# Running 20 of 23 expert tiles always, and the last three inside one branch

## The chip, the core and the metric

The kernel runs on one core of a Trainium2 chip. The metric is the device time of one execution in microseconds; the median of several runs is compared. The engines are called PE (matrix multiplication, with its weight loads shown as PEld), DVE (vector), ACT (scalar and activation), POOL (general purpose, here also the issuer of indirect transfers) and SP (the issuer of nearly all other transfers).

## What is computed

The reference is a two-layer decoder over x of shape (4, 256, 256), so 1024 rows of 256. Layer 0 is a windowed attention, a cross attention on 1601 context rows, and a ternary feed-forward block. Layer 1 is a latent attention, a linear cross attention and a mixture of experts. Each of the six blocks ends with a residual sum and a normalisation of each row. Only the last block matters here:

```
logits  = 30 * tanh((x @ w_gate) / 30)         # (1024, 8)
probs   = softmax(logits)
weights = probs, kept for the two largest of each row, 0 elsewhere
for e in range(8):
    h   = silu(x @ w1[e]) * (x @ w3[e])        # (1024, 512)
    out = out + (h @ w2[e]) * weights[:, e]    # (1024, 256)
x = layernorm(x + out)
```

Each row needs only two of the eight experts, so there are 2048 pairs of a row and an expert.

## The kernel before, in words

The kernel doesn't issue instructions as it is written. It records operations in a `Loom`, each with its engine, an estimated time, the buffers that it reads and writes and a priority. At the end `weave` puts them into one order by a small planner: of all operations that could go next, it takes the one that can start earliest, by the estimates, and on a tie the one of higher priority. That order is the order on each engine's queue. `hold_order(False)` lets the framework place the instructions that follow by its own rule until `hold_order(True)`. A buffer of a pool has a tag, and `room` and `take` hand out its places. Because all operations go through helpers, the profile shows most of them with the helper's line: L261 for matmuls, L268 for transposes, L275 for transfers issued by SP, L398 for DVE, ACT and POOL operations.

The mixture of experts is done by sorting rows into lists. After the cross attention of a batch, `route` finds each row's two experts, counts the rows of each expert in the running count `nxt`, and scatters the row (256 values, its gate and its slot) into the expert's list in DRAM (`lists`). A tile is 128 rows of one list. Since eight lists may each end with a partly filled tile, up to `TILES = 2 * T // P + NE - 1` = 23 tiles may be needed; how many really are depends on the routing. The kernel before always runs 23.

`tile_table` makes a table with one entry for each tile: an expert's number and the first row in its list. It is called three times. The first call, when three of the four batches have been routed, covers 5 tiles; the second, after seven eighths of the rows, 2 more; these two take only tiles that are already full. The last call covers the remaining `LATE` = 16. In it `nt` is the number of tiles that each expert still needs and `upto` its running sum over the experts; entries past the last needed tile point to rows that hold nothing.

`expert_tile` does one tile. Its steps are:

- on SP, a register load of the list's row from the table, and the fetch of the rows (`xg`, L1407 to L1409); a register load of the expert's number and two transfers with w1 and w3 of that expert (`wt`, 4 buffers, L1416 to L1421);
- on PE, a register load of the expert's number, two transposes of `xg` into a bank, copied to `xgT`; then matmuls of `xgT` with `wt` into two banks;
- tanh on ACT and two products on DVE, which give `eh`;
- on PE, matmuls of `eh` with `w2e`, which holds w2 of all experts, addressed with the expert's register;
- on DVE, the product with the gate (`ey`) and two small operations that give the rows' numbers (`slots`); then an indirect scatter by POOL into `yd` in DRAM (L1258). Rows that hold nothing go to spare rows of `yd`.

When all tiles are done, SP reads `yd` back (`back`, eight transfers), DVE adds it to the residual (`entry`), the rows are normalised with two small POOL operations for each batch (`rstd`), and SP writes the output.

Of the kernel before, what the change touches and what calls it, by code (L numbers as in the profile page):

```python
# [23 lines left out]
F32 = mybir.dt.float32  # L24
BF16 = mybir.dt.bfloat16
U32 = mybir.dt.uint32
I32 = mybir.dt.int32
AF = mybir.ActivationFunctionType
ALU = mybir.AluOpType
AX = mybir.AxisListType  # L30

P = 128
B, S, D = 4, 256, 256
# [7 lines left out]
NE, EI = 8, 512  # L41
# [5 lines left out]
class View:  # L47


    def __init__(self, buf, box, shape, steps=(), axes=None):  # L50
        self.buf, self.box, self.shape, self.steps, self.axes = buf, box, tuple(shape), steps, axes
        if axes is None and not steps:
            self.axes = tuple(range(len(self.shape)))
# [56 lines left out]
def meet(a, b):  # L110
    return a is None or b is None or all(x[0] < y[1] and y[0] < x[1] for x, y in zip(a, b))


def covers(a, b):
    return a is None or (b is not None and all(x[0] <= y[0] and y[1] <= x[1] for x, y in zip(a, b)))
# [22 lines left out]
class Pool:  # L138
# [2 lines left out]
        scope.pools.append(self)  # L141

    def tile(self, shape, dtype, tag, name=None, bufs=None, free=False, acc=False):
        g = self.groups.get(tag)
        if g is None:
            g = self.groups[tag] = Group(self, tag, bufs or self.bufs, free)
        b = Buf(g, list(shape), dtype, name or tag, acc)
        self.scope.bufs.append(b)
        return View(b, None, shape)
# [32 lines left out]
class Loom:  # L182
# [14 lines left out]
    def __init__(self, tc):  # L197
        self.tc, self.nc, self.ops, self.cur, self.prio, self.also = tc, tc.nc, [], None, (0,), []
        self.free = {"PE": 0.0, "DVE": 0.0, "ACT": 0.0, "POOL": 0.0, "SP": 0.0, "DMA": 0.0}
        self.vector, self.scalar, self.gpsimd = Side(self, "DVE"), Side(self, "ACT"), Side(self, "POOL")  # L200
        self.sync, self.order = self, None

    def hold_order(self, on):

        if self.order:
            self.order.__exit__(None, None, None)
        self.order = self.tc.manual_schedule() if on else None
        if on:
            self.order.__enter__()
# [6 lines left out]
        return op  # L216

    def op(self, ways, outs, ins, claims=(), after=(), size=None, land=1.6, what="", unordered=False):
        op = Op(ways, (*self.prio, len(self.ops)), what)
        op.size, op.land = size, land  # L220
        op.deps.update(after)
        op.deps.update(self.also)
        for v in ins:
            b = v.buf
            op.deps.update(o for box, o in b.writes if meet(box, v.box))
        for v in outs:
            b = v.buf
            if not unordered:
                op.deps.update(o for box, o in b.writes + b.reads if meet(box, v.box))
        for v in ins:  # L230
            v.buf.reads.append((v.box, op))
        for v in outs:
            b = v.buf
            if not unordered:
                b.writes = [(box, o) for box, o in b.writes if not covers(v.box, box)]
                b.reads = [(box, o) for box, o in b.reads if o is op or not covers(v.box, box)]
            b.writes.append((v.box, op))
        op.deps.discard(op)
        op.bufs = list(dict.fromkeys(v.buf for v in (*outs, *claims, *ins)))
        for b in op.bufs:  # L240
            b.left += 1
        self.ops.append(op)
        return op

    @contextmanager
    def piece(self, us, claims=(), ins=(), over=(), what=""):


        self.cur = ([], [], list(ins))
        yield  # L250
        fns, outs, ins = self.cur
        self.cur = None
        read = [o for v in over for _, o in v.buf.reads]
        self.op({"PE": (us, us, lambda: [f() for f in fns])}, outs, ins, claims, after=read, what=what)

# [169 lines left out]
def decoder(ctx: ExitStack, tc: tile.TileContext, a: dict, out: bass.AP):  # L425
    nc = tc.nc
    k = Loom(tc)
# [33 lines left out]
    p5, p5w = linear.pool("p5", 2), linear.pool("p5w")  # L461
    p4, p4w = causal.pool("p4", 2), causal.pool("p4w")
    own = [even.pool("p4even"), odd.pool("p4odd")]
    p6w = experts.pool("p6w")
    p6 = work.pool("p6", 3)

    def bank(shape=(P, 512), dtype=F32, acc=False):
        return psB.tile(shape, dtype, "bank", free=True, acc=acc)
# [24 lines left out]
    def at_prio(*prio):  # L493
        k.prio = prio
# [93 lines left out]
    for i in range(2):  # L588
        v = p1w.tile((P, 3, H // 2, 2, 32), F32, f"v{i}")
# [619 lines left out]
    EARLY[1] -= EARLY[0]  # L1209
    TILES = 2 * T // P + NE - 1  # L1210
    LATE = TILES - sum(EARLY)
    LISTS = (NE + 1) * T
    W = D + 2

# [3 lines left out]

    lists = in_dram((LISTS, W), "lists")
    yd = in_dram((2 * T + 1 + TILES * P, D), "yd")  # L1220

    def moe_prepare():
        pool, n = p5w, LISTS // P
        blank = p3.tile((P, FF), F32, "h")[:, :W]
# [13 lines left out]
        k.gpsimd.memset(onesb, 1.0)  # L1238
        iotaN = pool.tile((P, LATE), F32, "iotaN")
        iota(iotaN, 1)  # L1240
# [106 lines left out]
    def tile_table(n, before, last=False):  # L1347


        iotaN, start, nxt = state[4:]  # L1350
        tag = len(tables)

        def some(w, name):
            return p5.tile((P, w), F32, f"{name}{tag}", bufs=1)

        nt = some(NE, "nt")
        k.vector.tensor_scalar(nt, nxt, 1.0 / P, (127.0 if last else -127.0) / 256.0, ALU.mult, ALU.add)
        k.vector.tensor_scalar(nt, nt, MAGIC, MAGIC, ALU.add, ALU.subtract)
        st = start
        if before is not None:  # L1360
            st = some(NE + 1, "st")
            k.vector.tensor_copy(st, start)
            k.vector.tensor_tensor(st[:, :NE], st[:, :NE], before, ALU.add)
        k.vector.tensor_tensor(nt, nt, st[:, :NE], ALU.subtract)
        upto = some(NE, "upto")
        k.vector.tensor_copy(upto, nt)
        for e in range(1, NE):
            k.vector.tensor_tensor(upto[:, e : e + 1], upto[:, e : e + 1], upto[:, e - 1 : e], ALU.add)

        step = some(NE, "step")  # L1370
        k.vector.tensor_tensor(step, st[:, 1:], st[:, :NE], ALU.subtract)
        k.vector.tensor_tensor(step, step, nt, ALU.subtract)
        past = p5.tile((P, n, NE), F32, f"past{tag}", bufs=1)
        k.vector.tensor_tensor(
            past,
            upto.unsqueeze(1).to_broadcast([P, n, NE]),
            iotaN[:, :n].unsqueeze(2).to_broadcast([P, n, NE]),
            ALU.is_le,
        )
        ex, row = some(n, "ex"), some(n, "rowt")  # L1380
        k.vector.reduce_sum(ex, past, axis=AX.X)
        k.vector.tensor_tensor(past, past, step.unsqueeze(1).to_broadcast([P, n, NE]), ALU.mult)
        k.vector.reduce_sum(row, past, axis=AX.X)
        k.vector.scalar_tensor_tensor(row, row, st[:, 0:1], iotaN[:, :n], ALU.add, ALU.add)
        tab = p5.tile((P, 2, n), I32, f"tab{tag}", bufs=1)
        k.vector.tensor_scalar(tab[:, 0], ex, float(NE - 1), None, ALU.min)
        k.vector.tensor_scalar(tab[:, 1], row, float(P), None, ALU.mult)
        tables.append(tab)
        if last:
            return tab, None  # L1390

        taken = some(NE, "taken")
        k.vector.tensor_tensor(taken, nt, upto, ALU.subtract)
        k.vector.tensor_scalar(taken, taken, float(n), 0.0, ALU.add, ALU.max)
        k.vector.tensor_tensor(taken, taken, nt, ALU.min)
        if before is not None:
            k.vector.tensor_tensor(taken, taken, before, ALU.add)
        return tab, taken
# [3 lines left out]
    def expert_tile(i, tab, level):  # L1402
# [3 lines left out]
        def fetch():  # L1406
            row = nc.sync.value_load(tab.real()[0:1, 1, i : i + 1], min_val=0, max_val=LISTS - P)  # L1407
            k.hold_order(False)
# [55 lines left out]
        k.vector.tensor_tensor(slots, slots, slot, ALU.add)  # L1464
        scatter(yd, slots, y, 1.0, 2.0, "give")


    for b in range(B):
        at_prio(0, b)
# [39 lines left out]
    state, taken = moe_prepare(), None  # L1509
# [4 lines left out]
    w2 = p6w.tile((P, NE, 4, D), F32, "w2e")  # L1514
    for e in range(NE):
        k.dma_start(w2[:, e], rows(a["w2"][e]))
    level = 0
    for b in range(B):
        at_prio(7, b)
        for ts, x, xt in l1_attention(b):  # L1520
# [5 lines left out]
            if b == B - 1:  # L1526
                at_prio(8)
                n = EARLY[ts[0]]
                tab, taken = tile_table(n, taken)
# [5 lines left out]
            at_prio(7, b)  # L1535
        X[b] = xn
    at_prio(8)
    tab, _ = tile_table(LATE, taken, True)
    for i in range(LATE):
        expert_tile(i, tab, level)  # L1540
    for b in range(B):
        x = X[b]
        for e in range(2):
            y = p6.tile((P, 2, D), F32, "back", bufs=4)
            row0 = 1 + e * T + b * S
            k.dma_start(y, yd[row0 : row0 + S, :].rearrange("(t p) d -> p t d", p=P))
            k.vector.tensor_tensor(x, x, y, ALU.add)
        normalise(x)
        k.dma_start(out[b * S : (b + 1) * S, :].rearrange("(t p) d -> p t d", p=P), x)
# [72 lines left out]
```

## Time and profile before

| what | value |
|---|---|
| median of 3 runs | 708.22 us (708.21 to 709.07) |
| profiled execution, its own time | 710.24 us |
| profiled execution, span from first to last instruction | 708.5 us |
| granted PE clock, mean | 0.982 |
| PE busy | 664.6 us, 94% |
| DVE, ACT, POOL busy | 447.3 us (63%), 297.4 us (42%), 126.4 us (18%) |
| PE matmuls of `xgT` with `wt`, 23 tiles | 736, mean 278 ns |
| PE matmuls of `eh` with `w2e`, 23 tiles | 184, mean 380 ns |
| scatters by POOL into `yd` | 23, mean 971 ns |

The profile gives busy times of one execution, and the granted clock of PE. A row of the timeline has a start, a length, an engine, a line, an operation, the tiles written and read, and in brackets how long the engine was idle before it and what ended that. In the chain of waits each piece was released by the piece before it; its lengths add up to the time. The column SPq or POOLq is an engine's queue, issuing a transfer or waiting.

### The profile page before, as it was taken

To read this page: it belongs to the slowest core of one execution; us is meant where nothing else is said; L and a number is where in the kernel's file an instruction comes from. 1 tells how busy PE (TensorE), PEld (TensorE's weight loads), DVE (VectorE), ACT (ScalarE), POOL (GpSimd) and SP (SyncE) were. 2 spreads that over 40 slices of the span, in tenths; PEclk is the share of its full clock that TensorE was granted. 3 is DMA by queue.
4 is the path that set the end of the run, shared out by engine and by line. 5 is a ranking of instruction groups with operands and counts; after the bars stand their busy time and mean duration, and the time that the engine had idled before them with its cause. 6 is when DMAs were issued, how large, how long until landed. Compare 5 with 4: busy or idle time off the path is not lost.

```text
span 708.5 us, 12388 instructions
## 1 busy us (share of the span) xinstructions
PE 664.6 (94%) x4407; PEld 531.2 (75%) x4411; DVE 447.3 (63%) x1155; ACT 297.4 (42%) x930; POOL 126.4 (18%) x170
## 2 busy tenths in 40 slices
PE   7999999999999999999899999999998899999970
PEld 5787878568877777767676777767766898999960
DVE  4878896333528634384799978687686555333336
ACT  2868965211132433343358777476455121111100
POOL 3313223012300000000022011221213213111112
PEclk9999999999999999999999999999999999999995
DMA  8922100646998241000010600000002845976405
GB/s 302 351 76 76 52 19 10 205 128 224 331 300 283 67 149 37 1 1 1 0 54 1 237 3 1 1 31 1 30 1 73 318 147 195 364 278 228 147 26 177
DMA packets 62673, 87.33 MB, mean 123 GB/s; under 512 B 4654, under 2 KB 44340, under 8 KB 62612
## 3 DMA queue, kind: packets, MB, share of 16 engines
q1 hardware_dynamic: 60740, 81.40, 35.2%
q0 software_dynamic: 1872, 5.13, 2.0%
q8 instruction: 36, 0.59, 0.3%
q14 instruction: 25, 0.20, 0.1%
HBM read 70.83 MB, written 15.69 MB: 122 GB/s over the span
## 4 chain that ended last, share of the span: by engine, by line
PE 78%; DVE 14%; ACT 3%; DMA 2%; issue 1%; POOL 1%; SPq 0%; POOLq 0%; DVEq 0%
PE bank L261 70%; PE bank L268 8%; DVE at L398 3%; ACT at L398 3%; DVE nm L398 2%; DVE x L398 1%; DVE h L398 1%; POOL rstd L398 1%; DVE as L398 1%; DVE entry L398 1%; DVE st L398 1%; DMA wt<-in_w 1%; DMA back<-yd 1%; DVE kf L398 0%; DVE fm L398 0%
## 5 line engine op out<-in xcount | busy, mean ns | idle before, releaser
L398 ACT ACTIVATE at<-at,nm 128x128 f32<-128x128 f32 (+1 forms) x256 | 106.5, 420 | 25.7 <-DVE nm L398 25.2
L261 PE MATMUL bank<-xgT,wt 128*128 128x128 f32 x736 | 87.0, 278 | 0.8 <-DVE xgT L398 0.5
L261 PEld LDWEIGHTS bank<-xgT,wt 128*128 128x128 f32 x736 | 86.2, 195 | 2.0 <-DVE xgT L398 0.8
L268 PE MATMUL bank<-ident,at 128*128 128x128 f32 (+1 forms) x440 | 61.5, 277 | 1.8 <-DVE at L398 1.6
L268 PEld LDWEIGHTS bank<-ident,at 128*128 128x128 f32 (+1 forms) x440 | 50.8, 142 | 14.3 <-issue 5.9
L261 PE MATMUL bank<-V,aT 128*128 128x256 f32 (+1 forms) x240 | 55.2, 380 | 0.7 <-DVE o L398 0.6
L261 PE MATMUL bank<-KT,qT 128*128 128x512 f32 (+1 forms) x128 | 54.0, 553 | 0.0
L261 PEld LDWEIGHTS bank<-V,aT 128*128 128x128 f32 (+1 forms) x240 | 45.2, 190 | 11.2 <-issue 3.6
L398 POOL TENSOR_SCALAR rstd<-mv 128x2 f32<-128x2 f32 (+1 forms) x26 | 6.5, 251 | 261.6 <-DVE mv L398 215.8
L261 PE MATMUL bank<-kf,V 128*128 128x256 f32 (+1 forms) x208 | 50.4, 383 | 1.1 <-DVE kf L398 1.1
L398 DVE TENSOR_REDUCE nm<-at 128x4 f32<-128x512 f32 (+1 forms) x64 | 50.6, 807 | 0.4
L261 PE MATMUL bank<-wkv,KT 128*128 128x256 f32 (+1 forms) x208 | 49.7, 382 | 0.0
L398 ACT ACTIVATION_READ_ACCUMULATOR at<-at,nm 128x1 f32 x256 | 48.7, 190 | 0.0
L398 ACT ACTIVATE eh<-bank 128x512 f32<-128x512 f32 x23 | 13.7, 597 | 77.5 <-PE bank L261 77.5
L261 PEld LDWEIGHTS bank<-kf,V 128*128 128x128 f32 (+1 forms) x208 | 38.2, 190 | 7.5 <-DVE kf L398 2.3
L398 ACT COPY aT<-bank 128x512 f32<-128x512 f32 (+2 forms) x60 | 31.5, 551 | 29.4 <-PE bank L268 28.6
L261 PE MATMUL bank<-w2e,eh 128*128 x184 | 43.4, 380 | 0.0
L261 PEld LDWEIGHTS bank<-wkv,KT 128*128 128x128 f32 (+1 forms) x208 | 37.8, 186 | 7.3 <-issue 1.5
L398 DVE TENSOR_TENSOR at<-at,rs 128x512 f32<-128x512 f32 (+1 forms) x43 | 39.7, 924 | 0.8
L398 POOL TENSOR_TENSOR at<-at,rs 128x512 f32<-128x512 f32 (+1 forms) x21 | 23.6, 1123 | 87.9 <-DVE rs L398 74.7
L398 ACT ACTIVATE fm<-bank 128x512 f32<-128x512 f32 (+2 forms) x33 | 18.1, 552 | 46.6 <-PE bank L261 46.6
L1258 POOL DMA_INDIRECT yd<-ey,slots x23 | 22.3, 971 | 83.9 <-DVE slots L398 81.9
(246 smaller groups left out, 1231.3 us busy)
## 6 DMA issues: line engine op xcount, KB each, us to landing
wt<-in_w SPq DMA_DIRECT2D x46, 512.0 KB, 4.7
lists<-h SPq DMA_DIRECT2D x6, 1548.0 KB, 16.8
KT<-in_ctxT SPq DMA_DIRECT2D x6, 1024.0 KB, 5.1
V<-in_ctx SPq DMA_DIRECT2D x6, 1024.0 KB, 5.4
w2e<-in_w SPq DMA_DIRECT2D x8, 512.0 KB, 9.1
KT<-in_ctxT SPq DMA_DIRECT2D x6, 577.0 KB, 3.8
V<-in_ctx SPq DMA_DIRECT2D x6, 512.0 KB, 4.0
xg<-lists SPq DMA_DIRECT2D x23, 129.0 KB, 4.3
```

What stands on the lines that cost most here:

```text
L261: lambda: self.nc.tensor.matmul(real(o), real(lhsT), real(rhs), start=real(start), stop=stop, **kw)
L268: fns.append(lambda: self.nc.tensor.transpose(real(o), real(x), real(ident)))
L398: return getattr(engine, method)(*[real(x) for x in args], **{k: real(x) for k, x in kw.items()})
L1258: d = nc.gpsimd.indirect_dma_start(out=dst.real(), out_offset=bass.IndirectOffsetOnAxis(ap=row.real(), axis=0), in_=src.real(), in_offset= ...
```

## The change

The table of the last call gets a flag, `more`: 1 if more than `LATE - RARE` = 13 of its 16 tiles are needed, which is more than 20 of all 23. The first 13 late tiles are recorded as before. The last three become one recorded operation, `rare_tiles`, which comes after all operations recorded up to then. It loads the flag into a register of each of the five engines and opens a two-way switch on all of them: with 0 the arm is empty, with 1 it holds the three tiles, one after the other, in one set of buffers (`spare` and four `banks`). While that arm is emitted, `at_once` makes the recording helpers emit at once. The register loads, as the changed program stands, are placed by the framework just after the flag is made, ahead of most of the late tiles; the switch itself stands on each engine after the 20th tile's last instruction and before the reading back. In the empty arm each engine waits for its own earlier work and raises the semaphores that the skipped tiles would have raised.

```diff
     def tile(self, shape, dtype, tag, name=None, bufs=None, free=False, acc=False):
+        if self.scope.loom.at_once is not None:
+            return self.scope.loom.at_once[tag].pop(0)
...
     def op(self, ways, outs, ins, claims=(), after=(), size=None, land=1.6, what="", unordered=False):
+        if self.at_once is not None:
+            next(iter(ways.values()))[2]()
+            return None
...
     LATE = TILES - sum(EARLY)
+    RARE = NE // 2 - 1
...
         if last:
-            return tab, None
+            more = p5.tile((P, 1), I32, "more", bufs=1)
+            k.vector.tensor_scalar(more, upto[:, NE - 1 :], n - RARE + 0.5, None, ALU.is_gt)
+            return tab, more
...
+    def rare_tiles(tiles, tab, more, level):
+        spare = [
+            p5.tile((P, W), F32, "xg"), p6w.tile((P, 2, 2, EI), F32, "wt"), p6.tile((P, 2, P), F32, "xgT"),
+            p6.tile((P, EI // P, P), F32, "eh"), p6.tile((P, D), F32, "ey"), p5.tile((P, 1), I32, "slots"),
+        ]
+        banks = [bank((P, 2, P)), bank((P, EI // P, P)), bank((P, EI // P, P)), bank((P, D))]
+
+        def emit():
+            k.hold_order(False)
+            engines = (nc.tensor, nc.vector, nc.scalar, nc.gpsimd, nc.sync)
+            which = {e.engine: e.value_load(more.real()[0:1, 0:1], min_val=0, max_val=1) for e in engines}
+            for arm in tc.Switch(which, 2):
+                if arm:
+                    for i in tiles:
+                        k.at_once = {v.buf.group.tag: [v] for v in spare}
+                        k.at_once["bank"] = list(banks)
+                        expert_tile(i, tab, level)
+                        k.at_once = None
+            k.hold_order(True)
+
+        k.op({None: (0.0, 2.5, emit)}, [yd], [tab, more, w2], [*spare, *banks], after=[o for o in k.ops if o.bufs], unordered=True)
...
-    tab, _ = tile_table(LATE, taken, True)
-    for i in range(LATE):
+    tab, more = tile_table(LATE, taken, True)
+    for i in range(LATE - RARE):
         expert_tile(i, tab, level)
+    rare_tiles(range(LATE - RARE, LATE), tab, more, level)
```

More of the change, by code (lines that the diff above doesn't have):

```diff
@@ L201, in __init__ @@
         self.sync, self.order = self, None
+        self.at_once = None
     def hold_order(self, on):
@@ L252, in piece @@
         self.cur = None
+        if self.at_once is not None:
+            over = ()
         read = [o for v in over for _, o in v.buf.reads]
```

## The prediction

> **What bounds the kernel now.** I read the chain of waits first, from 560 us to the end. It is one engine until 686.20 us and a serial tail after that:
>
> ```profile
> 618.89 15.90 PE bank L261 x120
> 634.79 0.66 PE bank L268 x6
> 635.44 15.90 PE bank L261 x120
> 651.35 0.65 PE bank L268 x6
> 652.00 15.90 PE bank L261 x120
> 667.90 0.66 PE bank L268 x6
> 668.56 17.64 PE bank L261 x128
> 686.20 0.02 issue
> ...
> 687.25 2.40 DMA yd<-ey,slots
> ...
> 690.72 3.79 DMA back<-yd
> ```
>
> Columns are start, length, what. TensorE runs the expert tiles without a gap, three at a time: six transposes (0.66), then 120 matmuls (15.90). So three tiles take 634.79 - 618.23 = 16.56 us, and the next two groups 16.56 and 16.55. The second view, busy time by stretch, confirms that nothing else limits there:
>
> ```profile
> 618.20:634.80 16.60, 16.60 (x129) 15.93 (x128) 6.27 (x15) 2.72 (x6) 2.88 (x3) 1.00 0.80 270
> 634.80:651.30 16.50, 16.50 (x128) 15.83 (x127) 6.26 (x15) 2.72 (x6) 2.88 (x3) 1.00 0.71 241
> 686.20:708.50 22.30, 0.00 (x0) 0.00 (x0) 12.01 (x35) 0.00 (x0) 5.63 (x10) 0.57 0.48 153
> ```
>
> After the stretch and its length come PE, weight load, DVE, ACT and POOL busy, then granted clock, DMA share, GB/s. PE fills its stretches at clock 1.00; DVE, ACT and POOL are under half busy. The last 22.30 us have no matmul: they carry the last scatter, the reading back, and the normalisation. The third view is the timeline around the last table (577 to 602 us) and around the end:
>
> ```profile
> 588.34 0.68 DVE L398 TENSOR_TENSOR eh<-bank,eh 128x512 f32<-128x512 f32 x1
> 589.58 0.48 DVE L398 TENSOR_SCALAR ey<-bank,xg 128x256 f32<-128x256 f32 x1 [0.55 <-PE bank L261]
> 590.27 0.17 DVE L398 TENSOR_SCALAR tab<-rowt 128x16 int32<-128x16 f32 x1
> 597.08 3.81 PE L261 MATMUL bank<-xgT,wt 128*128 128x128 f32 x32 [0.29 <-DMA wt<-in_w]
> 601.62 3.84 PE L261 MATMUL bank<-xgT,wt 128*128 128x128 f32 x32 [0.52 <-DVE xgT L398]
> 687.25 0.96 POOL L1258 DMA_INDIRECT yd<-ey,slots  x1 [0.77 <-DVE slots L398]
> 692.46 1.49 DVE L398 TENSOR_TENSOR entry<-entry,back 128x512 f32<-128x512 f32 x2 [5.49 <-DMA back<-yd]
> ```
>
> The bracket is the engine's idle time before the row. The late table is a second critical place: its integers are ready at 590.35, SP then reads them and fetches weights, and PE waits 0.29 us for these at 597.08.
>
> [...] The trace shows the block: the instruction queue q8 moved 0.59 MB in 36 packets, 16.4 KB each. No row of it shows a stalled branch. [...]
>
> **Is the branch taken?** That depends on data, and the data are known. I worked out the reference's routing for the inputs that setup_inputs draws at its default seed: the eight experts get 328, 425, 248, 187, 259, 166, 230 and 205 rows. In tiles of 128, rounded up, that is 3+4+2+2+3+2+2+2 = 20. The whole tiles of the first 768 rows number 7, of the first 896 rows 10, so the early tables' 5 and 2 tiles are all real ones; the late table holds 20 - 7 = 13, and the flag asks for more than 13.5. It is 0. A 21st tile would need, say, expert 2 to gain 9 rows; only 2 of 1024 rows have second and third choices closer than 1e-4 in probability, 17 closer than 1e-3. So rounding on the chip won't set it.
>
> **The change, part by part.**
>
> 1. *Three tiles leave the main stream.* The program order keeps the same final pattern on PE (three transposes, an output piece, gate pieces, output pieces, with the last two output pieces back to back), with one whole group of three gone. Its price is a group's period: **-16.56 us**. With it go 3 row fetches and 6 weight DMAs on SP, 3 scatters on POOL (0.96 each), and 3 tanh, 9 large and 6 small DVE operations and 3 evacuations. All lay beside PE, so they add nothing more. The bound below this is zero: no tile-rate limit but PE shows.
>
> 2. *Making the flag.* One DVE operation on 128x1, 0.15 us by the slots row; it stands before the table's integers. Behind it DVE is busy until 589.02, then idles 0.55 us for PE before ey at 589.58. The idle time takes it: 0.
>
> 3. *Five register loads of the flag*, placed by the scheduler just after it. SP and PE already do such loads per tile: TENSOR_LOAD 268 and 302 ns, FUSED_REGOPS 152, SEQ_ASSERT 18, some 0.45 us together.
>  - SP reads it before the table's integers; the flag is ready from about 587, the integers at 590.35, so SP is idle then: 0.
>  - PE reads it after the second late tile's transposes, where it waits 0.52 us for xgT anyway: 0, at most 0.1.
>  - ACT and POOL: ACT was idle 4.70 us before the tanh behind it, POOL 2.70 us before its next scatter: 0.
>  - DVE is the delicate one. No DVE load is in the trace; I take PE's and SP's 0.45 plus five waits of about 20 ns that have long been satisfied, 0.55. It stands behind the eh product that ends at 589.02, and ahead of ey and both table conversions; SP's first late fetch and then PE at 597.08 wait for those. Idle there is 0.55 less the flag's 0.15, so 0.40. If the load starts only when the product has ended, 0.15 us pass through to PE; if it runs beside it (0.69 us long), nothing. I take **+0.1**, from 0 to 0.3.
>
> 4. *The dispatch and the empty arm, on each engine.* Stride constants, one register operation (0.15), an indirect branch[...], a prefetch hint, waits for the engine's own earlier work, additions to the semaphores that the skipped tiles would have raised, and a branch out over the second arm.
>  - SP gets there early: its weights for tile 20 went out by 645.3. Its arm waits for all eight of its DMA queues, so for these weights (4.7 us); PE needs another 20 us. Hidden.
>  - ACT's last tanh is some 5 us ahead of PE's end. PE has nothing after the branch but the final barrier. Hidden under the 22.30 us.
>  - DVE meets it after the last slots; behind it stands entry<-back, which has 5.49 us of idle ahead. Hidden, even with two block fetches of 2.1 to 2.4 us (estimated from the shortest DMAs here: out<-entry 2.1, yd<-ey 2.4).
>  - POOL is the only one with little cover. The first back DMA now waits for a semaphore that POOL's empty arm raises. POOL has issued the last scatter at 687.25 + 0.96 = 688.21, and the scatter lands at 689.65: 1.44 us. [...] **0**. [...] None can be a gain.
>
> Sum: -16.56 + 0.1 = -16.46. The profiled execution took 710.24 us with a span of 708.5; it becomes 693.8 with 692.0. The median of the three runs, 708.22, becomes **691.8**.
>
> **Rivals.**
>
> *The branch stalls on instruction fetch (faster, but less).* For: the arm's exit jumps over the other arm[...] and POOL's cover is only 1.44 us. [...] One fetch gives 691.8 + 1.4 = 693.2, two about 695.6; with a slower DVE load up to 696.
>
> *The branch is taken (slower).* If a 21st tile were asked for, the arm runs three tiles through one set of buffers, with nothing overlapped. The first has its weights ready: transposes 0.38, xgT 0.44, matmuls 3.73. Each of the next two waits for its weights behind the previous tile's matmuls: 0.94 issue + 4.7 landing + 3.73 = 9.4. The end adds tanh 0.60, products 0.7 + 0.7 and output matmuls 1.89, less overlap, about 3.4. Together 26.7 against 16.56 removed, and a fetch of 2.3 for the arm: 708.2 + 12.4 = about 720.6. It decides from 21 tiles on; the count above says 20. This is also the case in which the change does not do what it says.
>
> **How the numbers follow.** Hidden branch, 691.3 to 692.6: 0.60. Fetch or load on the path, to 697: 0.34. Something dearer but still a gain: 0.02. Taken, or a stall above 16 us: 0.04. The range 690.9 to 696 (its lower end is the point less 0.9, the spread of the three runs, 708.21 to 709.07) leaves out the last two and the upper end of the second. A measurement of this kernel tells some 0.2% (1.4 us) from no change: faster 0.95, same 0.01, slower 0.04.
>
> **What would show it.** The page should list 20 xgT,wt tiles (640 matmuls, not 736), 40 wt transfers and 20 scatters. The last matmul should end near 669.7, and the stretch from there to the end should be 22.3 us. A later last matmul puts the loss at the table (step 3: idle on PE before 597 grows). A longer tail puts it on the branch (step 4: look between POOL's last scatter and the first back DMA). 23 scatters would mean that the arm was taken and the prediction is wrong altogether.

## The result: faster by 12.3 us, with 4.2 us of the forecast gain missing

| | before | after |
|---|---|---|
| median of 4 runs each, us | 708.64 (708.21 to 709.94) | 696.81 (696.18 to 697.93) |
| ratio after / before, 95% interval | | 0.9827 (0.9815 to 0.9839) |
| span of the profiled execution, us | 708.5 | 694.7 |
| last matmul ends, us | 686.20 | 668.69 |
| from there to the span's end, "the tail", us | 22.30 | 26.01 |
| last scatter, from issue to landing, us | 2.40 | 4.95 |

The kernel is faster, as forecast, but the forecast was 691.8 us with a range up to 696.0. The two medians differ by 11.8 us. By the ratio, which the experiments below use too, the change takes 708.64 × 0.0173 = 12.3 us (11.4 to 13.1 by the interval); the prediction's sum was 16.46.

First the page of the kernel after: the expert group, and the queues that carry instructions (columns: packets, MB, share of 16 DMA engines).

```profile
L269 PE MATMUL bank<-xgT,wt 128*128 128x128 f32 x640 | 75.9, 279 | 1.4 <-DMA wt<-in_w 0.9
...
q8 instruction: 38, 0.62, 0.4%
q14 instruction: 38, 0.31, 0.2%
```

640 matmuls are 20 tiles, so the arm was not taken. Before, the same two queues had:

```profile
q8 instruction: 36, 0.59, 0.3%
q14 instruction: 25, 0.20, 0.1%
```

Although three tiles' work is gone, the changed kernel fetches more instructions, in pieces of 16 KB on q8 (0.62 MB in 38 packets) and 8 KB on q14 (0.31 MB in 38). Whose they are follows from counts in the trace of before. Its 12388 instruction records are 9181 of PE (matmuls, weight loads and its queue), 255 for each packet of q8, and 3207 of the other four engines, 128 for each packet of q14. From these counts q8 is read as bringing PE's instructions, and q14 those of the others.

Next the busy time by stretch, after (stretch and length; PE, weight load, DVE, ACT and POOL busy; clock, DMA share, GB/s):

```profile
617.72:634.28 16.56, 16.56 (x129) 15.89 (x127) 6.27 (x16) 2.66 (x7) 2.88 (x3) 1.00 0.81 274
...
668.69:694.70 26.01, 0.00 (x0) 0.00 (x0) 12.01 (x35) 0.00 (x0) 5.62 (x10) 0.60 0.44 135
```

The steady stream is as before, 16.56 us for three tiles. In the tail DVE and POOL work as long as before, 12.01 and 5.62 us, but it is 3.7 us longer. The chain of waits after (start, length, what) shows where:

```profile
669.74 4.95 DMA yd<-ey,slots
674.69 0.02 SPq L283
...
674.85 0.40 SPq L283
675.25 0.06 issue
675.31 1.70 SPq L283
677.01 0.05 issue
677.06 3.10 DMA back<-yd
```

And SP's first two back DMAs before:

```profile
689.79 0.37 SPq L275
...
690.21 0.46 SPq L275
```

Before, the scatter landed 2.40 us after its issue and the second back DMA took SP 0.46 us; now it is 4.95 and 1.70. Adding up from the last matmul: to the scatter's issue 1.05 us in both; landing +2.55; SP's first back DMA 0.16 behind it (0.14); from there to the first entry<-back on DVE 3.62 (2.67), so +0.95; the rest 16.23 (16.04), so +0.2. Together 3.7.

The timeline at the last table, after:

```profile
587.47 0.69 DVE L406 TENSOR_TENSOR eh<-bank,eh 128x512 f32<-128x512 f32 x1 [0.59 <-PE bank L269]
587.82 3.73 PE L269 MATMUL bank<-xgT,wt 128*128 128x128 f32 x32
588.99 0.48 DVE L406 TENSOR_SCALAR ey<-bank,xg 128x256 f32<-128x256 f32 x1 [0.83 <-DVE eh L406]
589.68 0.17 DVE L406 TENSOR_SCALAR tab<-rowt 128x16 int32<-128x16 f32 x1
596.13 3.81 PE L269 MATMUL bank<-xgT,wt 128*128 128x128 f32 x32 [0.90 <-DMA wt<-in_w]
```

PE's gate piece (its matmuls of `xgT` with `wt`), before:

```profile
589.38 3.73 PE L261 MATMUL bank<-xgT,wt 128*128 128x128 f32 x32
```

Before, ey followed the start of PE's gate piece by 0.20 us (589.38, 589.58); now by 1.17. PE waits 0.90 us for weights (0.29), and its gap from one gate piece to the next is 8.31 us, not 7.70: +0.6. So in the two profiled executions: tiles −16.55, table +0.6, tail +3.7, and −1.6 that was there before the table (the gate piece starts at 587.82, not 589.38). That last term is not put down to the change: across the traces of all the kernels here this point lies between 587.8 and 591.2. Without it the sum is −12.25, close to the 12.3 of the ratio.

### The profile page after: what moved, and what is told of

It is laid out like the page before. It is cut to its first block, busy times and chain, and to the rows that moved or that the text cites. A ratio compares the mean times of both kernels' runs of the same rounds, so it can differ in the third digit from the quotient of the medians.

```text
span 694.7 us, 12093 instructions
## 1 busy us (share of the span) xinstructions
PE 646.5 (93%) x4281; PEld 514.7 (74%) x4285; DVE 441.5 (64%) x1141; ACT 294.3 (42%) x924; POOL 123.4 (18%) x167
## 4 chain that ended last, share of the span: by engine, by line
PE 66%; DVE 14%; issue 11%; ACT 4%; POOL 3%; DMA 2%; SPq 0%; POOLq 0%; DVEq 0%
PE bank L269 58%; PE bank L276 8%; DVE at L406 4%; ACT at L406 3%; DVE nm L406 2%; POOL yd L1267 2%; DVE x L406 1%; DVE h L406 1%; POOL rstd L406 1%; DVE as L406 1%; DVE entry L406 1%; DVE st L406 1%; DMA yd<-ey,slots 1%; DVE kf L406 0%; DMA back<-yd 0%
## 5 line engine op out<-in xcount | busy, mean ns | idle before, releaser
L269 PE MATMUL bank<-xgT,wt 128*128 128x128 f32 x640 | 75.9, 279 | 1.4 <-DMA wt<-in_w 0.9
L269 PEld LDWEIGHTS bank<-xgT,wt 128*128 128x128 f32 x640 | 75.1, 195 | 2.5 <-issue 1.3
L406 ACT ACTIVATE eh<-bank 128x512 f32<-128x512 f32 x20 | 11.9, 597 | 67.9 <-PE bank L269 60.0
L406 POOL TENSOR_TENSOR at<-at,rs 128x512 f32<-128x512 f32 (+1 forms) x21 | 23.5, 1121 | 86.9 <-DVE rs L406 73.6
L269 PE MATMUL bank<-w2e,eh 128*128 x160 | 37.8, 380 | 0.0
L406 DVE TENSOR_REDUCE m<-bank 128x1 f32<-128x512 f32 (+1 forms) x32 | 20.5, 640 | 25.8 <-PE bank L269 25.6
```

The costliest lines, as they stand in the source:

```text
L269: lambda: self.nc.tensor.matmul(real(o), real(lhsT), real(rhs), start=real(start), stop=stop, **kw)
L406: return getattr(engine, method)(*[real(x) for x in args], **{k: real(x) for k, x in kw.items()})
```

## The experiments

Why is the last scatter late? There were three theories. **Theory 1**: POOL's empty arm makes up for the skipped scatters (an INC_SWDGE_SEM, 920 ns, at 670.4) and SP must wait for that. **Theory 2**: engines that branch fetch blocks of instructions through the same DMA engines that carry the scatter and the first back DMAs. **Theory 3**: POOL's own branch holds its scatter up. Each kernel's ratio is to the kernel before on the same chip (before had medians of 709.69, 710.81 and 709.26 us in the three groups, so ratios are compared, not times).

| kernel | ratio (95%) | scatter's landing, us | tail, us |
|---|---|---|---|
| before | 1 | 2.40 | 22.3 |
| after | 0.9827 (0.9815 to 0.9839) | 4.95 | 26.0 |
| e1_twenty | 0.9766 (0.9750 to 0.9782) | 2.39 | 22.9 |
| e2_noscatter | 0.9825 (0.9807 to 0.9842) | 5.39 | 26.5 |
| e3_flaglater | 0.9800 (0.9780 to 0.9820) | 5.58 | 27.4 |
| f1_free | 0.9819 (0.9803 to 0.9835) | 5.27 | 25.8 |
| g1_nope | 0.9798 (0.9778 to 0.9819) | 3.53 | 23.5 |
| g2_nopool | 0.9838 (0.9817 to 0.9860) | 4.72 | 25.4 |
| f3_swapped | 0.9809 (0.9789 to 0.9830) | 5.17 | 26.3 |
| f4_best | 0.9876 (0.9854 to 0.9897) | 2.53 | 28.3 |
| h1_traffic | 0.9775 (0.9758 to 0.9792) | 3.44 | 23.6 |
| g3_sponly | 0.9767 (0.9748 to 0.9786) | 2.39 | 22.6 |
| e4_loadsonly | 1.0000 (0.9992 to 1.0008) | 2.40 | 22.3 |
| e5_taken | 1.0413 (1.0390 to 1.0435) | 3.79 | 24.9 |

Landing and tail are from one profiled execution each; the ratios are from 4 to 13 runs. A single landing is still telling: it is 2.39 to 2.53 us in five kernels (before, e1_twenty, f4_best, g3_sponly, e4_loadsonly), and 4.72 to 5.58 in the six that have PE in the switch, send the last scatter ahead of it and don't take the arm. Before, in e1_twenty and in g3_sponly no instruction packet starts beside the last scatter; in f4_best one of q8 does, after 679.08 us, when 46 of the scatter's 48 packets have started; e4_loadsonly has no switch.

### e1_twenty: the tiles alone

```diff
-            more = p5.tile((P, 1), I32, "more", bufs=1)
-            k.vector.tensor_scalar(more, upto[:, NE - 1 :], n - RARE + 0.5, None, ALU.is_gt)
-            return tab, more
+            return tab, None
...
-    rare_tiles(range(LATE - RARE, LATE), tab, more, level)
```

> 20 tiles, with no flag and no switch at all (complete for these inputs, which need 20). Theory: removing three tiles is worth one group's period, 16.56 us, and everything else that is missing from the forecast is the switch and its loads. So 708.6 - 16.6 = 692.1, last matmul to end 22.3 us as before. Rival: part of the loss comes from the shorter stream itself (weights or reading back arrive worse); then 694 to 696 and a tail above 23 us.

Measured: 0.9766, which is 708.64 × 0.0234 = 16.6 us. So three tiles are worth what the prediction's step 1 said, and flag, loads and switch together cost 708.64 × 0.0061 = 4.3 us, give or take 1.4 by the two intervals. Landing 2.39, as before, and a tail of 22.9: the rival of a shorter stream that runs worse falls.

### e2_noscatter: no scatter in the arm

```diff
-        scatter(yd, slots, y, 1.0, 2.0, "give")
+        if k.at_once is None:
+            scatter(yd, slots, y, 1.0, 2.0, "give")
```

> As the changed kernel, but the second arm has no scatters (it is not run for these inputs), so that POOL's empty arm raises no semaphore of the indirect queue. Theory 1: the 2.55 us by which the first back transfer starts later come from INC_SWDGE_SEM on POOL, for whose effect SP waits; then the wait from POOL's last scatter to SP's wake-up falls from 4.95 to about 2.4 us and the time is 696.8 - 2.55 = 694.2. Theory 2 (rival): the scatter itself lands later, because instruction blocks are being fetched for the branch; then 4.95 stays and so does 696.8.

The three tiles of the arm that isn't taken leave out their scatter, so POOL's empty arm has no INC_SWDGE_SEM. Measured: 0.9825 and a landing of 5.39. Nothing is won; Theory 1 falls.

### e3_flaglater: the flag made after the sixth late tile

```diff
-            return tab, more
+            return tab, upto
...
+        slots = expert_tile(i, tab, level)
+        if i == 5:
+            k.vector.scalar_tensor_tensor(more, upto[:, NE - 1 :], LATE - RARE + 0.5, slots, ALU.is_gt, ALU.min)
```

> As the changed kernel, but the flag is made from the sixth late tile's slots, so that the register loads stand in the steady stream and not ahead of the table. Theory 1: the DVE load (541 + 222 + 31 ns and five waits) is what delays the table; PE's second matmul group after the table then waits 0.3 us for weights instead of 0.9, and 0.6 us are won: 696.2. Rival: the delay on DVE begins before the load (the eh product already starts 0.68 us late), from an instruction fetch; then the table stays late and 696.8 stays.

The slots operand only holds the operation back. Measured: ey starts 0.21 us after the gate piece again (589.13, 588.92), with no DVE idle before it, and PE's gap is 7.84 us. The eh product is late here too (it starts 0.41 us before the gate piece), so it is the load behind it that delays ey, and the rival of an earlier delay falls. The delay of ey is gone; the tail is not mended (landing 5.58, and 27.4 us in all). The ratio 0.9800 is better than the changed kernel's 0.9827, but the intervals overlap; the difference, 1.9 us, is more than the 0.6 that the trace explains. Of the versions that can still run 23 tiles it has the lowest ratio, but its interval doesn't set it apart from f3_swapped, f1_free or the changed kernel.

### f1_free: reading back without waiting for the arm

```diff
+            if k.at_once is not None:
+                rare_given.append(d.ins)
...
-            k.dma_start(y, yd[row0 : row0 + S, :].rearrange("(t p) d -> p t d", p=P))
+            read_back(y, yd[row0 : row0 + S, :].rearrange("(t p) d -> p t d", p=P))
```

`read_back` is the same DMA without the dependency on the arm's scatters; in the arm SP waits for them itself.

> As the changed kernel, but the reading back does not wait for the arm's scatters; in the second arm SP itself waits for them with one transfer that reads yd. POOL's INC_SWDGE_SEM still runs in the empty arm. Theory 1: what costs is SP's wait for that instruction's semaphores, not POOL's time in it, so 694.2 as with the scatters left out. Theory 2 (rival): the scatter lands late whatever waits for it; 696.8.

Measured: 0.9819, landing 5.27. SP no longer waits for anything of POOL's empty arm, and the first back DMA still comes only when the 20th tile's own scatter has landed. This refutes Theory 1 a second time.

### g1_nope and g2_nopool: fewer engines in the switch

```diff
-            engines = (nc.tensor, nc.vector, nc.scalar, nc.gpsimd, nc.sync)
+            engines = (nc.vector, nc.gpsimd, nc.sync)
```

and for g2_nopool `(nc.tensor, nc.vector, nc.scalar, nc.sync)`. In both, the arm that isn't taken leaves out the work of the missing engines.

> Only DVE, POOL and SP stand in the switch; in the second arm, which is not run for these inputs, the operations that need PE or ACT are left out or replaced by memsets. The last scatter landed after about 5 us instead of 2.4 even where nothing waited for POOL's semaphores. Theory 2, block fetches: the branches set off instruction transfers on the same DMA engines as the scatter (4 packets of 16 KB on q8 and 7 of 8 KB on q14 around the branch, against 1 before), and PE's 16 KB ones are the slow part; its exit branch ends just when the scatter lands. Without PE in the switch the landing falls to 2.4 to 3.5 us and the time to about 694.5. Theory 3, POOL's own branch holds up its descriptors: the landing stays near 5 us and the time at 696.8.

> PE, DVE, ACT and SP in the switch, POOL not; the scatters are left out of the second arm. Theory 2, block fetches, mainly PE's: the landing stays at 4.5 to 5.5 us and the time at about 696.5. Theory 3, POOL's branch: the landing is 2.4 us and the time about 694.

Without PE (and ACT) in the switch the landing falls to 3.53 us and the tail to 23.5; without POOL it stays at 4.72 and 25.4. So it is not POOL's branch: Theory 3 falls. g1_nope is the stronger witness, for POOL keeps both its branches there and the landing falls all the same; in g2_nopool POOL still has one branch record (0.04 us at 672.54, just before the scatter). In g1_nope q8 has no packet beside the scatter; in g2_nopool it has two. What g1_nope leaves, 1.1 us above the 2.39 to 2.40 of a kernel with no switch, is not PE's.

### f3_swapped: the empty arm second

```diff
-                if arm:
+                if not arm:
...
-            k.vector.tensor_scalar(more, upto[:, NE - 1 :], n - RARE + 0.5, None, ALU.is_gt)
+            k.vector.tensor_scalar(more, upto[:, NE - 1 :], n - RARE + 0.5, None, ALU.is_lt)
```

> The whole changed kernel with the arms in the other order: the flag is 1 when 20 tiles are enough, so that the empty arm is the second one and the code after the switch follows it directly. Theory 2: PE's far fetch then starts at its dispatch, some 3 us earlier, when the last scatter is not yet on its way, and the way out is the next block; the landing falls to 3 to 4 us, 695 to 696. If PE's fetches have nothing to do with it, no change: 696.8.

Measured: 0.9809, landing 5.17, PE's two branch instructions 3.47 and 4.60 us. In the time as a whole, which arm stands first makes no difference that these runs can tell; either way PE's branches take 2.8 us or more, and instruction packets run beside the scatter. So Theory 2's forecast for this run, 3 to 4 us, missed. It took PE's blocks to be out of the way by then, which was an estimate, and they are not: two q8 packets (673.286 to 674.646 and 674.193 to 676.215) still run beside the scatter that is issued at 672.06. The wait of the other engines moves, though. After, with the empty arm next in sequence, ACT, DVE, POOL and SP go on 0.41 to 0.50 us after the first branch; here, with the long arm jumped over, it is 2.45, 2.89, 2.81 and 5.02 us.

### f4_best: the last scatter behind the switch

It joins f3_swapped's order and e3_flaglater's flag, and holds scatters back, of which in the end only the last one stands behind the switch:

```diff
+        slots, give = expert_tile(i, tab, level, i >= LATE - RARE - 2)
...
+    held.append(rare_tiles(range(LATE - RARE, LATE), tab, more, level))
+    for give in gives:
+        give()
```

> The whole changed kernel, with the arms swapped, the flag made after the sixth late tile, and the last scatter (with its DVE steps) placed after the switch on POOL and DVE. The far fetches of POOL and DVE then come before that scatter. Theory 2: landing near 2.4 us, but POOL and DVE may come late to the last scatter by one fetch, 1 to 2 us; 694 to 696. Theory 3: the landing is 2.4 us since POOL's branch is over; the same time or better, 693.5 to 695.

A failed attempt at a better version (699.9 us by the ratio, where 694 to 696 was expected), with a telling timeline:

```profile
669.95 0.96 POOL L1267 DMA_INDIRECT yd<-ey,slots  x1 [4.34 <-DVE slots L406]
676.06 0.48 DVE L406 TENSOR_SCALAR ey<-bank,xg 128x256 f32<-128x256 f32 x1 [6.39 <-issue]
...
677.08 0.96 POOL L1267 DMA_INDIRECT yd<-ey,slots  x1 [6.17 <-DVE slots L406]
```

DVE's two branches in the same run (duration ns min/median/max; first and last start, us):

```profile
L1666 DVEq COMPARE_BRANCH  x2: 60/68/75, 669.8 to 673.4; - x2
```

The last ey, too, came to stand behind DVE's switch, and DVE idles 6.39 us before it with nothing that the profile shows to wait for. The branches themselves are recorded with 60 and 75 ns; DVE's queue stands still for 3.4 us after the first and 2.4 us after the second. These waits now lie on the path (0.9876, the slowest of the gains). But the scatter that goes out when they are over lands in 2.53 us. That is what Theory 2 asks for.

### h1_traffic: the suspected cost by itself

Twenty tiles, no flag, no switch, and one useless transfer of 32 rows of 8 KB beside the last scatter:

```diff
+    extra = p6w.tile((P, 2, 2, EI), F32, "wt")
+    k.vector.tensor_scalar(extra[:, 0, 0, 0:1], slots, 1.0, None, ALU.mult)
...
+            out=extra.real()[0:32].rearrange("p a b n -> p (a b n)"),
+            in_=a["w1"][0].rearrange("(p r) n -> p (r n)", r=4)[0:32, :],
```

> Twenty tiles, with no flag and no branch, as in e1_twenty; and one extra transfer by SP of 32 rows of 8 KB (0.26 MB, to a buffer that nobody reads), released when the last tile's slots are made, so that it runs beside the last scatter. It puts the suspected cost by itself: large packets on the DMA engines at that moment, with no instruction fetched. Theory 2 (the fetched instruction blocks keep the scatter and the first back transfers waiting for DMA engines): the last scatter lands 1 to 2.5 us later than in e1_twenty (2.39 us from issue), so at 3.4 to 5 us, and the ratio to the kernel before is 0.978 to 0.980 beside e1_twenty's 0.9766. If the delay has to do with the branch itself (semaphores of the empty arm, engines that stop) and not with DMA traffic: landing near 2.4 us, ratio 0.9766.

Landing 3.44 us, 1.05 more than in e1_twenty, at the lower edge of what Theory 2 expected. The ratio, 0.9775, doesn't tell it from e1_twenty's 0.9766: 0.6 us is less than either interval allows. So large packets alone, with no branch anywhere, did delay this scatter, by 1.05 us in this execution. The useless transfer moves more than the instruction blocks do (0.26 MB), so it shows that such a delay occurs, not how large that of the blocks must be.

### g3_sponly: the switch on SP alone

```diff
-            engines = (nc.tensor, nc.vector, nc.scalar, nc.gpsimd, nc.sync)
+            engines = (nc.sync,)
```

> The switch stands on SP alone, and only SP loads the flag; PE, ACT, DVE and POOL run twenty tiles with no branch (in the arm that isn't taken, SP would only fetch). Theory 2: SP branches at about 645 us, 20 us before the end, so its fetches are over by the last scatter; landing 2.4 to 2.6 us, tail 22.5 to 23.2 us, and no late table, since DVE loads nothing: ratio 0.976 to 0.979. If the wait comes from SP's own arm (its queues' waits, its jump over the other arm): landing or the first back issue near the 5.1 us of the changed kernel, ratio near 0.982.

Measured: 0.9767, landing 2.39, tail 22.6, like e1_twenty without any switch. SP's switch costs nothing that these runs can tell; SP reaches it some 20 us ahead of the last matmul. The trace shows one short branch on each of the other engines as well (0.03 to 0.19 us, at 645.6 to 647.2), equally far ahead.

### What the DMA queues show

The queues tell more than the landing does. The last scatter is 48 packets on q0. In e1_twenty, from 670.5 to 672.0 (1.0 to 2.5 us after the last scatter's start at 669.47 us; columns as above, share within the window):

```profile
q0 software_dynamic: 48, 0.13, 25.1%
```

All 48 are done, and no other queue starts anything. After, from 671.0 to 672.0 us:

```profile
q0 software_dynamic: 39, 0.11, 39.3%
q8 instruction: 1, 0.02, 12.0%
q14 instruction: 1, 0.01, 9.9%
```

and after, from 672.0 to 674.5:

```profile
q0 software_dynamic: 9, 0.02, 6.2%
q14 instruction: 1, 0.01, 1.9%
```

A packet counts where it starts. 39 of the 48 have started at the usual time, 2.3 us after the issue. The other nine trickle in over the next 2.2 us, although most of the DMA engines' time is free (the shares are 6.2 and 1.9%, and two instruction packets that started earlier add 5%). So the DMA as a whole was not short of bandwidth there; by the packets below, a few of its engines were held up. Counted in the same way, from 2.5 us after the issue, 2 packets are late in g1_nope and 12 in e2_noscatter, none in f4_best, g3_sponly and e1_twenty. In h1_traffic, where the extra packets are spread, 14 of the 16 engines' shares end 0.3 to 0.9 us later, counted from the issue, than the last one in e1_twenty.

The trace also holds each packet's start, length and size, and these say what the held-up packets wait for. The 48 packets, 32 of 4096 bytes and 16 of 4 bytes, are read as a share of three for each of 16 DMA engines: two large ones, then a small one. In before and e1_twenty none of the 32 large ones takes over 0.21 us, and all 16 shares are over by 2.1 us after the issue. After, 12 shares are over by then too; in the four others the large packets take 0.27 to 1.09 us each. Where two packets of a share follow each other undisturbed, the second starts some 3 ns before the end of the first. Much the same is seen across queues: in each of the eight kernels with a switch and a late landing, the share that ends last takes up a packet 3 to 74 ns before the end of an instruction packet:

| kernel | instruction packet, us | queue | packet of the last share starts, us |
|---|---|---|---|
| after | 671.357 to 672.945 | q14 | 672.872 |
| e2_noscatter | 673.011 to 674.630 | q14 | 674.561 |
| e3_flaglater | 671.978 to 674.254 | q8 | 674.250 |
| f1_free | 672.400 to 673.891 | q14 | 673.817 |
| g1_nope | 674.890 to 675.623 | q14 | 675.620 |
| g2_nopool | 674.847 to 676.467 | q8 | 676.453 |
| f3_swapped | 674.193 to 676.215 | q8 | 676.212 |
| e5_taken | 715.598 to 716.826 | q8 | 716.823 |

So a part of the scatter is read as queueing behind an instruction block, and the landing waits for it: it comes 0.5 us behind the last packet after, and 0.3 to 0.4 before. The block may be PE's (q8) or another engine's (q14): after, another q8 packet ends at 673.071 and a held-up share starts at 673.057, but the share behind the q14 packet ends last. The first back DMAs tell the same: from landing to the first entry<-back it is 2.8 to 2.9 us in the five kernels with no switch near the end, 3.0 to 3.2 in f4_best, e5_taken and g1_nope, and 3.7 to 4.8 in the other six.

Who asks for the blocks is read from the line of the switch, after (duration ns min/median/max; first and last start, us):

```profile
L1653 PEldq COMPARE_BRANCH  x2: 2820/3547/4274, 666.8 to 670.1; - x2
...
L1653 DVEq COMPARE_BRANCH  x2: 60/68/75, 669.6 to 670.3; - x2
L1653 POOLq COMPARE_BRANCH  x2: 43/52/60, 669.7 to 671.3; - x2
```

PE's sequencer runs ahead of its matmuls here: it meets the switch at 666.8 us, where the last matmul ends at 668.69. It spends 2.8 and 4.3 us in its two branches, the second across nearly the whole flight of the last scatter. A q8 packet starts at 667.163 us, beside the first branch, and two beside the second, at 670.379 and 671.145. In the other runs too there is a wait at a branch: 2.8 to 4.8 us in PE's, and 2.45 to 5.02 us behind the first branch of the other engines in f3_swapped. So the wait is read as one for a fetch by DMA, and the held-up shares add that this DMA has neighbours. What stays inferred: no record says which branch asked for an instruction packet, or names the DMA engine of a packet. That a held-up share and an instruction block were on the same one is read from the times above, and from g1_nope, f4_best and h1_traffic. Nor is it shown how the delay divides between PE's blocks and those of DVE, ACT and POOL beyond g1_nope, which took PE and ACT out together.

### e4_loadsonly: steps 2 and 3 alone

```diff
-            for arm in tc.Switch(which, 2):
...
-    for i in range(LATE - RARE):
+    for i in range(LATE):
```

> All 23 tiles as in the kernel before, with the flag and its five register loads (their values are not used) and no switch. It measures the prediction's steps 2 and 3 alone. By the prediction: +0.1 us (0 to 0.3), ratio 1.0000 to 1.0004. By the traces of the changed kernel, in which DVE's load ends about 0.6 us behind the old start of ey: +0.6 us, ratio 1.0008; the row ey in the trace has 0.8 us of idle that a DVE operation ends, in place of 0.55 that PE ends. If the late table were a matter of the run and not of the load: ratio 1.000 and ey with 0.55 us of idle ended by PE.

Measured: 1.0000 (0.9992 to 1.0008), so 0 ± 0.6 us. The timeline around the load:

```profile
587.23 0.68 DVE L406 TENSOR_TENSOR eh<-bank,eh 128x512 f32<-128x512 f32 x1
588.25 3.73 PE L269 MATMUL bank<-xgT,wt 128*128 128x128 f32 x32
588.78 0.48 DVE L406 TENSOR_SCALAR ey<-bank,xg 128x256 f32<-128x256 f32 x1 [0.87 <-PE bank L269]
```

Here the eh product ends 0.34 us before PE's gate piece, and ey follows that piece by 0.53 us. After, the product waited 0.59 us for PE and began only 0.35 us before the gate piece, and the same load made ey follow by 1.17. The load's cost depends on how late DVE is at that moment (in e1_twenty the product is late as well, at no cost to ey, since no load follows it). Six kernels with a late product and the load (after, e2_noscatter, f1_free, f3_swapped, g1_nope, g2_nopool) have ey 1.14 to 1.24 us behind, and 8.15 to 8.85 us from one gate piece to the next; in the other eight that is 7.25 to 8.05. The lateness need not be a property of the program: e5_taken differs from the changed kernel in one constant, and in its profiled execution the product starts 1.03 us ahead of the gate piece, ey follows by 0.51 and the gap is 7.62 us. So my expectation of +0.6 missed for this kernel; for the changed one 0.6 is what one execution shows, and no comparison of times isolates it.

### e5_taken: the rival on the other side

```diff
-            k.vector.tensor_scalar(more, upto[:, NE - 1 :], n - RARE + 0.5, None, ALU.is_gt)
+            k.vector.tensor_scalar(more, upto[:, NE - 1 :], n - RARE - 0.5, None, ALU.is_gt)
```

> The changed kernel with its threshold lowered by one, so that a need of 20 tiles already takes the branch: the same three tiles of rows that hold nothing run in the arm, one after the other in one set of buffers. The prediction's rival on the other side: 708.2 + 12.4 = 720.6 us, ratio 1.0175, with some 26.7 us from the 20th tile's last matmul to the arm's last scatter. If the fetch of the long arm is dearer than the 2.3 us taken (the arm holds some 150 PE instructions, and each engine that enters it fetches): 722 to 728 us, ratio 1.02 to 1.028.

Measured: 1.0413, or 737.9 us for the 708.64 of before; the rival said 720.6 and the wider expectation at most 728. The timeline says why:

```profile
673.68 0.66 PE L276 MATMUL bank<-ident,xg 128*128 128x128 f32 x2 [4.23 <-issue]
...
684.21 0.35 SPq L1420 DMA_DIRECT2D xg<-lists  x1
...
689.41 5.22 PE L269 MATMUL bank<-xgT,wt 128*128 128x128 f32 x32 [2.40 <-DMA wt<-in_w]
...
703.63 6.58 PE L269 MATMUL bank<-xgT,wt 128*128 128x128 f32 x32 [2.73 <-DMA wt<-in_w]
```

Entering the arm costs PE 4.2 us. The next tile's rows are fetched at 684.21, when the previous tile's slots (683.92 + 0.16) have released xg; the weights stand behind that fetch on SP, though their buffer was free 3.7 us earlier. So it is 14.2 to 14.6 us from one tile's matmuls to the next, not 9.4. And between such pauses the clock that PE is granted is 0.56 to 0.72 in these matmul groups: 5.2 to 6.6 us for the 3.73 assumed. That the pauses lower the clock is not tested here.

## Why the prediction was right and where it failed

- **Step 1 was right.** e1_twenty gives 16.6 us, the trace 16.55, predicted 16.56. The data count held too: 20 tiles, flag 0, 20 scatters. The last matmul came at 668.69 rather than near 669.7: +0.6 of table and −1.6 from before the table.
- **Step 2 was right.** The flag's operation is 0.15 us and is hidden.
- **Step 3 failed on one engine, in size.** On SP, ACT, POOL and PE the loads are hidden. For DVE the prediction took PE's and SP's 0.45 us, plus five waits of 20 ns: 0.55 in all. The trace has 541 + 222 + 31 ns, and five waits of 50 ns:

```profile
L1489 DVEq EVENT_SEMAPHORE  x5: 49/50/50, 587.5 to 587.9; - x5
...
L1489 DVEq TENSOR_LOAD <-more x1: 541/541/541, 588.0 to 588.0; - x1
```

 From 587.5 to 588.86 that is 1.35 us. The load did begin beside the product, as the prediction hoped, but was twice as long as it. Instead of +0.1 (at most 0.3) the trace of this execution shows about +0.6; e4_loadsonly and e5_taken, where the product was early, show none of it between the gate pieces (7.63 and 7.62 us, 7.70 before).
- **Step 4 failed, and with it the forecast.** Its term for dispatch and arm was 0; the tail grew by 3.7 us. "PE has nothing after the branch but the final barrier. Hidden" is true of PE's time and wrong of its effects. The prediction priced a fetch only as a stall of the engine that branches, and so looked at POOL, whose cover it found thin. POOL's own part was hidden: from its first branch at 669.70 to the end of its second at 671.38 it takes 1.7 us (0.43 of wait behind the first branch, 0.92 of INC_SWDGE_SEM), and with the 2.40 us of before the scatter would have landed at 672.1. The 0 for POOL's branch was the author's estimate; the trace of before has no branch to show it. And POOL is not what SP waits for (e2_noscatter, f1_free, g2_nopool). In place of that stall, other transfers are held up beside the instruction packets: 2.55 us on the scatter and 0.95 on the first back DMAs. 1.4 of the 2.55 go when PE and ACT, which have no work left after the branch, are taken out of the switch; what g1_nope leaves ends behind a q14 packet.
- **What a branch took.** PE's first branch took 2.8 us; the other engines went on 0.41 to 0.50 us after theirs. Their branches are recorded with 43 to 75 ns, PE's with 2.8 to 4.8 us. But the short records are not the whole price: on those four engines a wait stands behind the branch, 2.45 to 5.02 us in f3_swapped, and 3.4 and 2.4 us on DVE in f4_best.
- **The rival "stalls on instruction fetch" was nearest**, 695.6 us for two fetches and up to 696 with a slow DVE load. Its amount for two fetches, 3.8 us above the forecast's point, was the author's estimate and near the truth by chance, for its place, POOL's path, was wrong. The rows that the prediction named for finding the fault, the stretch between POOL's last scatter and the first back DMA, were the right ones. The text let this case reach 697 and then ended the range at 696.0, where the table's and the tail's loss add up to 4.3.
- **The rival "taken" had the right sign and less than half the size**: 12.4 us over before, measured 29.3. It missed that xg's release orders the weights, and the lower clock that PE had in the arm.

## What to carry to other kernels

In this kernel a branch was paid for by the transfers that ran beside its instruction packets (2.55 us on the scatter, 0.95 on the first back DMAs), more than by the engine that branched: before calling a branch on an idle engine free, ask which transfer that others wait for is in flight at that moment. One late share was enough: in g1_nope 15 of the scatter's 16 were over within 2.2 us, and the landing still came 1.1 us late. If a switch is needed, let its fetches fall into a stretch where transfers have slack (g3_sponly's switch, 20 us ahead of the last matmul, left a landing of 2.39 us), and keep a register load out of a chain that an engine is already late in (after, ey came 1.17 us behind the gate piece; in e4_loadsonly, with DVE earlier, 0.53).

## What the runs showed of the hardware that was not expected

- A register load from a tile, TENSOR_LOAD of the flag, took 276 ns on SP, 385 on PE, 541 on DVE, 618 on ACT and 633 on POOL after; the register operation behind it took 151 to 222.
- PE's compare-and-branch took 2.8 to 4.8 us each in the seven kernels that have PE in the switch and don't take the arm. The other engines' are recorded with 43 to 75 ns, and the next instruction followed 0.41 to 0.50 us later after, where the arm that is taken stands first, and 2.45 to 5.02 us later in f3_swapped, where it stands second.
- In eight kernels the last share of the scatter took up a packet 3 to 74 ns before the end of an instruction packet: after, two shares began 1.4 and 1.6 us behind the last of the others, while most of the DMA engines' time was free (shares of 6.2 and 1.9%).
- PE's granted clock in the matmul groups of e5_taken's arm, where it pauses for 2.4 to 4.2 us again and again, was 0.56 to 0.72, where the steady stream has 1.00.
